# Two cross-attentions on one core: weights and x laid out in long runs, a bias row loaded early, and the last rounds shared out anew

## The chip, the cores and the metric

The kernel runs on one core of a Trainium2 chip. The metric is the device time of one execution in microseconds (us). The median of three runs of the kernel before the change is 1020.93 us (1020.56 to 1021.36).

## The reference

Two attention layers run one after the other, each with its residual and layer norm. There are 2 batches of 2048 tokens with 512 features, and a context of 128 tokens per batch. Both layers have 16 heads; layer 0 has 64 features per head (1024 in all), layer 1 has 32. All is float32.

```python
def layer0(x, ctx, mask):
    q = x @ Wq + bq;  k = ctx @ Wk + bk;  v = ctx @ Wv + bv          # 16 heads of 64
    a = (q . k) * mask
    a = exp(a - max(a over everything)) * mask
    a = a / (sum(a over keys) + 1e-15)
    return layernorm((a . v) @ Wo + bo + x) * gamma + beta

def layer1(y, ctx):
    q = y @ Wq.T;  k = ctx @ Wk.T;  v = ctx @ Wv.T                   # 16 heads of 32
    a = softmax(q . k / sqrt(32) over keys)
    return layernorm((a . v) @ Wo.T + bo + y) * gamma + beta

out = layer1(layer0(x, ctx, mask), ctx)
```

## The kernel before

The 4096 tokens are cut into eight blocks t = 0 to 7 of TB = 512 tokens (four to a batch). NQ = 4 row tiles of 128 tokens make a block, and NG = 4 groups g of four heads make the heads. The order of the work is written out by hand: each engine (PE for matmuls, DVE, ACT, POOL, and SP, which issues nearly all transfers) runs its own queue in the order of the program, so an instruction that waits holds up all behind it on its engine.

**Buffers.** A pool hands out its buffers of one tag in turn; a tile that takes a buffer waits until the last reader of the tile that had it is done. Tags that matter here: "q" (4 buffers of 128x512: queries, later the reciprocal rows r, and before the change the row bo1), "z" (8 buffers: value biases bv0, the sums t1, t2, t4 of tokens, later the residual rows), "mm" and "av" (two PSUM banks each), "sc0" and "sc1" (two double banks of PSUM for scores and maxima).

**The opening (L208 to L254).** The transposed context cT goes out on ACT's queue, the key weights wk0, x and the query weights wq0 on SP's, the masks on POOL's. The weights come from DRAM as 128-row chunks of their rows. Layer 0's weights wk0 and wq0 are fetched in parts, because the first groups are needed first; `load_x(t)` fetches the transposed block t in two halves. `row` (L131) fetches a row and spreads it over 128 partitions.

**Layer 0's steps (L477 to L532).** i = 0 to 15 runs over pairs of blocks p and groups g. Each step makes queries of two blocks for one group, and their scores; the probabilities and values of the step before come in between. `keys0(e)` makes the keys of two heads (e = 0 to 7, two of them per group). At i = 0 the queries are four plain products (`queries0`, L329); from i = 1 on `queries_pair` (L348) makes four query tiles with seven products out of sums of weights and tokens, and DVE adds them up (L360, L362). `scores0` (L396) multiplies with keys and DVE (L408) masks and takes a maximum; each maximum goes to DRAM ("top") and comes back spread over all partitions ("every"). `exponentials0` reduces it on DVE, takes the exponential on ACT (L433), and masks on POOL (L434). `attend0` sums (den, L444) and multiplies with values (psu, L452). At i = 4 the weights of layer 1's keys and values are fetched, and then this:

```python
                bo1s = row(four, bo1, "bo1", "q")
                nc.gpsimd.tensor_tensor(b0s, b0s, bo1s, ALU.add)
```

The bias of layer 1's output is thus folded into the beta of layer 0, which the residual of layer 1 goes through.

**Rounds (L878 to L932).** From then on `steps(t)` lists what round t does, for t = -1 to 7. Letters stand for functions: X `maxima` (L693), M `turn_maxima` (L736), S `scores1` (L766, in the last round also L773), P1 `exponentials1` (L790), V `attend1` (L809), C `divide1` (L820), E `project1` (L831), Y `rest1` (L838, adds the residual), I `moments1`, O `norm1` (ACT L846, POOL L849 and L852), W `store` (L868); T `turn` (L662), Q `queries1` (L680) and Pr `project0` (L629) belong to the next block's layer 0 and queries. In the lists n = t + 1, l = t - 1. `moments1` calls `statistics` (L608): bn on DVE, rstd on POOL (L616), and, if scaled, a shift on POOL (L621). Round 6 makes the queries of block 7, the scores of block 6, and projects rows 0 and 1 of block 5. Round 7 has no next block: it projects rows 2 and 3 of block 5 and all rows of block 6 between the maxima and the scores of block 7.

**The last rows (L949 to L963).** Block 7's four rows are projected, the first half of the groups for all rows first. Row 0 is normed by ACT (`whiten1`) and POOL (`gamma1`, `beta1`), rows 1 to 3 by two DVE operations each (`norm1_vector`, L861 and L864).

Of the kernel before, what the change touches and what calls it, by code (L numbers as in the profile page):

```python
# [9 lines left out]
F32 = mybir.dt.float32  # L10
# [6 lines left out]
P = 128  # L17
# [7 lines left out]
def two_cross_attentions(  # L25
# [29 lines left out]
    K = maskT.shape[1]  # L55
    E = wq0.shape[1]
    H = 16
# [62 lines left out]
    wide = const.tile([P, 2 * ND, TB], F32, tag="wide", name="wq0")  # L120
    wq0s = wide.rearrange("p c m -> p (c m)").rearrange("p (c m) -> p c m", c=ND)

    def chunks(w):
        return w.rearrange("(c p) m -> p c m", p=P)

    def columns(pool, v, name, queue=nc.sync):
        sb = pool.tile(list(v.shape), F32, tag=name, name=name)
        queue.dma_start(sb, v)
        return sb
# [75 lines left out]
    with tc.tile_pool(name="w1", bufs=1) as w1, tc.tile_pool(name="a2", bufs=2) as a2, tc.tile_pool(  # L205
# [3 lines left out]
        first = w1.tile([P, 2 * ND, TB], F32, tag="first", name="wk0")  # L209
        wk0s = first.rearrange("p c m -> p (c m)").rearrange("p (c m) -> p c m", c=ND)  # L210
        W = 2 * P

        for c in (slice(0, 2), slice(2, 4)):
            nc.scalar.dma_start(cTs[:, c, :], chunks(cT)[:, c, :])
            nc.sync.dma_start(wk0s[:, c, :P], chunks(wk0)[:, c, :P])
        nc.sync.dma_start(wk0s[:, :, P : 2 * P], chunks(wk0)[:, :, P : 2 * P])
        nc.sync.dma_start(wk0s[:, :, 2 * P : 4 * P], chunks(wk0)[:, :, 2 * P : 4 * P])
        bk0s = columns(w1, bk0, "bk0", nc.scalar)
        bq0s = columns(w1, bq0, "bq0", nc.scalar)

        def load_x(t):

            b, q0 = where(t)
            pool, tag = (big, "big") if t // 2 % 2 else (xs, "xt")
            tiles = []
            for h in range(2):
                xt = pool.tile([P, 2, TB], F32, tag=tag, name=f"xt_{t}_{h}")
                rows = xT[b, 2 * h * P : 2 * (h + 1) * P, q0 : q0 + TB]
                nc.sync.dma_start(xt, rows.rearrange("(c p) q -> p c q", p=P))
                tiles.append(xt)  # L230
            xts[t] = tiles
# [8 lines left out]
        masks = {0: load_mask(0), 1: load_mask(1)}  # L240
        load_x(0)
        wv0s = []
        for n in range(E // W):
            at = slice(n * W, (n + 1) * W)
            if n == 1:
                load_x(1)
                for c in range(ND):
                    w = big.tile([P, 2, TB], F32, tag="big", name=f"wv0_{c}")
                    wv0s.append(w.rearrange("p n q -> p (n q)"))
                    nc.sync.dma_start(wv0s[c], wv0[c * P : (c + 1) * P, :])  # L250
                bv0s = [row(eight, bv0[:, n * TB : (n + 1) * TB], f"bv0_{n}", "z") for n in range(E // TB)]
            nc.sync.dma_start(wq0s[:, :, at], chunks(wq0)[:, :, at])
            if n > 1:
                nc.sync.dma_start(wk0s[:, :, at], chunks(wk0)[:, :, at])  # L254

# [3 lines left out]
        def keys0(e):  # L259
            ps = mm_tile(f"psk0_{e}")  # L260
            for c in range(ND):
                nc.tensor.matmul(  # L262
                    ps[:, : B * K], wk0s[:, c, e * P : (e + 1) * P], cTs[:, c, :],
                    start=(c == 0), stop=(c == ND - 1),
                )
# [21 lines left out]
        def halves0(g):  # L287
            return [
                [wq0s[:, 2 * k : 2 * k + 2, (2 * g + m) * P : (2 * g + m + 1) * P] for k in range(2)]
                for m in range(2)  # L290
            ]
# [34 lines left out]
        def queries0(t, e):  # L326
            ps = mm_tile(f"psq0_{t}_{e}")
            for c in range(ND):
                nc.tensor.matmul(  # L329
                    ps, wq0s[:, c, e * P : (e + 1) * P], xts[t][c // 2][:, c % 2, :],  # L330
                    start=(c == 0), stop=(c == ND - 1),
                )
# [129 lines left out]
        bo0s, g0s, b0s = row(const, bo0, "bo0"), row(const, g0, "g0"), row(const, b0, "b0")  # L462
        g1s, b1s = row(const, g1, "g1"), row(const, b1, "b1")
        b0cs = columns(const, b0c, "b0c")
        g0cs = columns(const, g0c, "g0c")
# [11 lines left out]
        for i in range(len(order) // 2):  # L477
            p, g = i // NG, i % NG
            steps0 = order[2 * i : 2 * i + 2]
            if g == (2 if p == 0 else 1) and p + 1 < NB // 2:  # L480
                for t in (2 * p + 2, 2 * p + 3):
                    load_x(t)
                    masks[t] = load_mask(t)
            if p == 0 and g != 1:
                for e in range(4) if g == 0 else (2 * g, 2 * g + 1):
                    keys0(e)
# [3 lines left out]
            if i == 4:  # L490
                w = w1.tile([P, 2 * ND, TB], F32, tag="first", name="wkv1")
                wk1s, wv1s = w[:, :ND, :], w[:, ND:, :]
                nc.sync.dma_start(wk1s, chunks(wk1))
                nc.sync.dma_start(wv1s, chunks(wv1))
                bo1s = row(four, bo1, "bo1", "q")
                nc.gpsimd.tensor_tensor(b0s, b0s, bo1s, ALU.add)
            if i == 12:
# [380 lines left out]
    def steps(t):  # L878
        n, f, l = t + 1, t + 2, t - 1
        if n == NB:  # L880
            return [
                (X, t, 0), (V, l, 3), (E, l - 1, 2), (Y, l - 1, 2), (I, l - 1, 2), (X, t, 1), (E, l - 1, 3),
                (Y, l - 1, 3), (I, l - 1, 3), (O, l - 1, 2), (X, t, 2), (E, l, 0), (Y, l, 0), (I, l, 0),
                (O, l - 1, 3), (W, l - 1, 2), (X, t, 3), (E, l, 1), (M, t), (Y, l, 1), (I, l, 1), (O, l, 0),
                (W, l - 1, 3), (E, l, 2), (Y, l, 2), (I, l, 2), (O, l, 1), (W, l, 0), (S, t, 0), (E, l, 3),
                (Y, l, 3), (I, l, 3), (O, l, 2), (W, l, 1), (S, t, 1), (V, t, 0), (C, t, 0), (O, l, 3),
                (W, l, 2), (S, t, 2), (V, t, 1), (C, t, 1), (S, t, 3), (V, t, 2), (C, t, 2), (W, l, 3),
                (V, t, 3), (C, t, 3),
            ]
# [30 lines left out]
        if n == NB - 1:  # L920
            return start + [
                (T, n), (M, t), (O, l, 0), (Q, n, 0), (O, l, 1), (Q, n, 1), (S, t, 0), (P1, t, 0),
                (Q, n, 2), (S, t, 1), (P1, t, 1), (V, t, 0), (W, l, 0), (Q, n, 3), (S, t, 2), (P1, t, 2),
                (V, t, 1), (W, l, 1), (S, t, 3), (P1, t, 3), (V, t, 2),
            ]
# [26 lines left out]
    for i in range(NQ):  # L952
        project1(t, i, 1)
        if i == 1:
            whiten1(t, 0)
            gamma1(t, 0)
        rest1(t, i)
        moments1(t, i, i == 0)
    beta1(t, 0)
    for i in (0, 3, 1, 2):  # L960
        if i:
            norm1_vector(t, i)
        store(t, i)  # L963
# [52 lines left out]
```

## Time and profile before

| | |
|---|---|
| median of three runs | 1020.93 us |
| profiled execution | 1018.7 us, its span 1016.9 us |
| mean granted clock of PE | 0.991 |
| PE busy | 984.1 us, 97% of the span |
| DVE, POOL, ACT busy | 619.3, 471.6, 385.4 us |
| DMA | 127.12 MB, 125 GB/s in the mean |
| chain that ended last | PE 84%, DVE 6%, issue 4%, DMA 3%, ACT 2%, POOL 1% |

All views come from one profiled execution; its times are us from the start of the span. A timeline line reads: start, busy time, engine, line of the kernel, operation, output <- inputs, shapes, count, and in brackets the idle time of that engine just before with what ended it. A line of the waits reads: who waited <- for whom: total us, times, longest us. A line of the window table reads: stretch, its length, the busy time (and count) of PE, of PE's weight loads, of DVE, ACT and POOL, then the clock that PE was granted (1.00 is full), the share of the 16 DMA engines that was busy, and the GB/s moved. PEq, SPq and so on are the queues that issue.

### The profile page before, as it was taken

The page shows a single profiled execution, that of the slowest core. Times are in us where ns is not written, and L with a number is a line of the kernel's source. Part 1 is how long each engine was busy: PE and PEld are TensorE (multiplying, and loading weights), DVE is VectorE, ACT ScalarE, POOL GpSimd, SP SyncE. Part 2 cuts the span into 40 slices and gives each one's busy share as a digit, 9 for nine tenths or more (in the row PEclk, how much of TensorE's full clock was granted, in tenths as well). Part 3 has the DMA queues.
Part 4 walks back from the last instruction along what each step waited for, and adds up shares of the span by engine and source line. Part 5 has one row for each costly group of instructions (what it writes and reads, how often), then busy time and mean ns, then how long its engine had stood idle before and what let it go on. Part 6 is the DMA issues. An engine that isn't in the chain of part 4 may idle for free.

```text
span 1016.9 us, 12273 instructions
## 1 busy us (share of the span) xinstructions
PE 984.1 (97%) x4484; PEld 423.8 (42%) x4484; DVE 619.3 (61%) x965; ACT 385.4 (38%) x622; POOL 471.6 (46%) x392
## 2 busy tenths in 40 slices
PE   8999969999999999999999999999999999999895
PEld 5444323333333334464544444344344344343332
DVE  2544634565564454149569569579488497595767
ACT  1133324333344344134434433434444344344250
POOL 0043244444334445692624925826736547443152
PEclk9999979999999999999999999999999999999998
DMA  9324244214232533642632632713714624204111
GB/s 332 123 53 156 54 140 136 79 53 148 62 79 58 162 120 122 202 134 73 253 121 83 235 99 85 269 64 110 267 64 154 215 85 183 91 1 178 63 53 41
DMA packets 56427, 127.12 MB, mean 125 GB/s; under 512 B 9424, under 2 KB 18384, under 8 KB 52784
## 3 DMA queue, kind: packets, MB, share of 16 engines
q1 hardware_dynamic: 54384, 123.72, 36.3%
q0 software_dynamic: 1152, 2.10, 0.7%
q8 instruction: 35, 0.57, 0.2%
q10 hardware_dynamic: 832, 0.53, 0.2%
q14 instruction: 24, 0.20, 0.1%
HBM read 100.15 MB, written 26.18 MB: 124 GB/s over the span
## 4 chain that ended last, share of the span: by engine, by line
PE 84%; DVE 6%; issue 4%; DMA 3%; ACT 2%; POOL 1%; SPq 0%; POOLq 0%; ACTq 0%; DVEq 0%
PE pso L629 21%; PE ps L348 15%; PE pso L831 10%; PE psq_None L680 8%; PE st L396 6%; PE psu L452 5%; PE mx L693 3%; PE s L766 3%; PE den L444 3%; PE u L809 3%; PE psq L680 2%; PE psq L329 1%; PE psv L274 1%; PE psk L262 1%; DVE p L785 1%
## 5 line engine op out<-in xcount | busy, mean ns | idle before, releaser
L434 POOL TENSOR_TENSOR sm<-sm,mask 128x1024 f32<-128x1024 f32 x64 | 150.1, 2369 | 212.7 <-ACT sm L433 212.7
L629 PE MATMUL pso<-wo,uT 128*128 128x512 f32 x512 | 229.3, 599 | 0.4 <-POOL uT L181 0.4
L616 POOL TENSOR_TENSOR rstd<-rstd,mhalf 128x1 f32<-128x1 f32 x64 | 35.7, 558 | 253.3 <-DVE shift L620 251.9
L629 PEld LDWEIGHTS pso<-wo,uT 128*128 128x128 f32 x512 | 94.3, 190 | 120.7 <-issue 115.3
L831 PE MATMUL pso<-wq,ctx 128*128 128x512 f32 x256 | 114.7, 599 | 0.0
L408 DVE CUSTOM_DVE_ANT_1 sm<-st,mask 128x1024 f32<-128x1024 f32 x64 | 75.9, 1222 | 52.2 <-PE st L396 31.0
L785 DVE TENSOR_TENSOR p<-s,p 128x1024 f32<-128x1024 f32 x56 | 66.0, 1219 | 60.8 <-PE s L766 53.4
L709 ACT ACTIVATE e<-mx,less 128x128 f32<-128x128 f32 x224 | 61.0, 383 | 103.8 <-DVE less L706 103.8
L433 ACT ACTIVATE sm<-sm,ncs 128x1024 f32<-128x1024 f32 x64 | 69.8, 1139 | 72.9 <-DVE ncs L430 72.7
L360 DVE TENSOR_TENSOR q<-ps,q 128x512 f32<-128x512 f32 x75 | 51.5, 689 | 68.8 <-ACT sm L433 31.7
L680 PE MATMUL psq_None<-yT,wq 128*128 128x512 f32 x192 | 88.4, 604 | 1.1 <-ACT yT L669 1.1
L348 PE MATMUL ps<-xt,wq 128*128 128x512 f32 x180 | 83.4, 599 | 0.0
L790 ACT ACTIVATE p<-p 128x2048 f32<-128x2048 f32 x28 | 53.5, 1911 | 73.1 <-DVE p L785 38.7
L181 POOL TENSOR_TENSOR uT<-uT,r 128x1024 f32<-128x1024 f32 x32 | 75.1, 2358 | 6.6 <-DMA r<-r 6.0
L396 PE MATMUL st<-q,k 64*128 64x512 f32 x256 | 65.1, 624 | 8.2 <-DVE q L360 8.0
L831 PEld LDWEIGHTS pso<-wq,ctx 128*128 128x128 f32 x256 | 46.8, 190 | 57.1 <-issue 50.9
L723 DVE TENSOR_REDUCE sums<-e 128x16 f32<-128x2048 f32 x28 | 63.8, 2277 | 1.1 <-ACT e L717 1.1
L452 PE MATMUL psu<-sm,v 128*32 128x512 f32 x512 | 64.1, 607 | 0.0
L699 DVE TENSOR_REDUCE tops<-mx 128x8 f32<-128x1024 f32 x32 | 39.1, 1222 | 29.7 <-PE mx L693 29.7
L348 PE MATMUL ps<-t,s 128*128 128x512 f32 x120 | 56.4, 592 | 0.0
L446 ACT COPY dens<-den 128x512 f32<-128x512 f32 x32 | 18.8, 588 | 98.5 <-PE den L444 98.5
L680 PEld LDWEIGHTS psq_None<-yT,wq 128*128 128x128 f32 x192 | 34.6, 189 | 51.0 <-issue 46.0
(127 smaller groups left out, 1332.2 us busy)
## 6 DMA issues: line engine op xcount, KB each, us to landing
p<-rows SPq DMA_DIRECT2D x28, 1024.0 KB
u<-u SPq DMA_DIRECT2D x32, 512.0 KB
uT<-u SPq DMA_DIRECT2D x32, 512.0 KB
xt<-in_xT_dram SPq DMA_DIRECT2D x16, 512.0 KB
z<-in_x_dram SPq DMA_DIRECT2D x32, 256.0 KB
r<-r SPq DMA_DIRECT2D x32, 256.0 KB
out_dram<-y SPq DMA_DIRECT2D x32, 256.0 KB
r<-rows SPq DMA_DIRECT2D x28, 256.0 KB
```

The costliest lines, as they stand in the source:

```text
L181: nc.gpsimd.tensor_tensor(u, u, r.unsqueeze(1).to_broadcast([P, 2, TB]), ALU.mult)
L348: nc.tensor.matmul(ps, w[:, c, :], x[c] if isinstance(x, tuple) else x[:, c, :], start=(c == 0), stop=(c == 1),)
L396: nc.tensor.matmul(st[n][:, j, :], k0[rows, 2 * g + n, b * K : (b + 1) * K], q[rows, :], start=True, stop=True,)
L408: nc.vector.tensor_tensor_reduce(out=sm, in0=st[n], in1=masks[t].unsqueeze(1).to_broadcast([P, 2, TB]), scale=1.0, scalar=-3.4028234e38, o ...
L433: nc.scalar.activation(s, s, AF.Exp, bias=ncs[:, i + n : i + n + 1])
L434: nc.gpsimd.tensor_tensor(s, s, masks[t].unsqueeze(1).to_broadcast([P, 2, TB]), ALU.mult)
L452: nc.tensor.matmul(ps[32 * j : 32 * (j + 1), :], v0[:, b, d : d + 32], p[j], start=True, stop=True,)
L629: nc.tensor.matmul(ps, uTs[t, n // 2][:, n % 2, i * P : (i + 1) * P], wo0s[n // 2][:, n % 2, :], start=(n == 0), stop=(n == NE - 1),)
L680: nc.tensor.matmul(ps[:, at], wq1s[:, c, g * P : (g + 1) * P], yTs[t][:, c, at], start=(c == 0), stop=(c == ND - 1),)
L723: nc.vector.tensor_reduce(to.rearrange("p r i o -> p r (i o)"), open_x.pop((t, g)), AX.X, ALU.add)
L785: nc.vector.tensor_tensor(p1[:, at], ps[n], p1[:, at], ALU.subtract)
L831: nc.tensor.matmul(ps, ctxs[t][:, g, i * P : (i + 1) * P], wo1s[:, g, :], start=(g == 0), stop=(g == NG - 1),)
```

## The change

1. The host lays out wk0 and wq0 by group of 256 columns, x by block and half, cT by partition, so that one transfer of a partition is one run: 2 KB (wk0 group 0 in halves, cT) or 4 KB (the other weight groups, x) instead of 512 bytes, 1 KB or 2 KB. In SBUF the weights lie group by group.
2. Ahead of the first queries only group 0 of wk0 is fetched and only keys 0 and 1 are made; keys 2 and 3 are made at i = 1.
3. The row bo1 is fetched before x(1), into a "z" buffer, and added before the first step.
4. Rows 2 and 3 of block 5 are projected in round 6; round 6 turns the maxima before it turns the next block; round 7 has two projections fewer.
5. Of block 7, rows 0 and 1 are normed by ACT and POOL, rows 2 and 3 by DVE.

```diff
     wide = const.tile([P, 2 * ND, TB], F32, tag="wide", name="wq0")
-    wq0s = wide.rearrange("p c m -> p (c m)").rearrange("p (c m) -> p c m", c=ND)
+    wq0s = wide.rearrange("p c m -> p (c m)").rearrange("p (n c m) -> p n c m", n=NG, c=ND)
...
-        W = 2 * P
         for c in (slice(0, 2), slice(2, 4)):
-            nc.scalar.dma_start(cTs[:, c, :], chunks(cT)[:, c, :])
-            nc.sync.dma_start(wk0s[:, c, :P], chunks(wk0)[:, c, :P])
-        nc.sync.dma_start(wk0s[:, :, P : 2 * P], chunks(wk0)[:, :, P : 2 * P])
-        nc.sync.dma_start(wk0s[:, :, 2 * P : 4 * P], chunks(wk0)[:, :, 2 * P : 4 * P])
+            nc.scalar.dma_start(cTs[:, c, :], cT[:, c, :])
+            nc.sync.dma_start(wk0s[:, 0, c, :], wk0[:, 0, c, :])
...
-                rows = xT[b, 2 * h * P : 2 * (h + 1) * P, q0 : q0 + TB]
-                nc.sync.dma_start(xt, rows.rearrange("(c p) q -> p c q", p=P))
+                nc.sync.dma_start(xt, xT[b, q0 // TB, h])
...
         load_x(0)
+        nc.sync.dma_start(wq0s[:, 0], wq0[:, 0])
+        bo1s = row(eight, bo1, "bo1", "z")
+        load_x(1)
         wv0s = []
-        for n in range(E // W):
-            at = slice(n * W, (n + 1) * W)
-            if n == 1:
-                load_x(1)
-                for c in range(ND):
-                    w = big.tile([P, 2, TB], F32, tag="big", name=f"wv0_{c}")
-                    wv0s.append(w.rearrange("p n q -> p (n q)"))
-                    nc.sync.dma_start(wv0s[c], wv0[c * P : (c + 1) * P, :])
-                bv0s = [row(eight, bv0[:, n * TB : (n + 1) * TB], f"bv0_{n}", "z") for n in range(E // TB)]
-            nc.sync.dma_start(wq0s[:, :, at], chunks(wq0)[:, :, at])
-            if n > 1:
-                nc.sync.dma_start(wk0s[:, :, at], chunks(wk0)[:, :, at])
+        for c in range(ND):
+            w = big.tile([P, 2, TB], F32, tag="big", name=f"wv0_{c}")
+            wv0s.append(w.rearrange("p n q -> p (n q)"))
+            nc.sync.dma_start(wv0s[c], wv0[c * P : (c + 1) * P, :])
+        bv0s = [row(eight, bv0[:, n * TB : (n + 1) * TB], f"bv0_{n}", "z") for n in range(E // TB)]
+        for n in range(1, NG):
+            nc.sync.dma_start(wk0s[:, n], wk0[:, n])
+            nc.sync.dma_start(wq0s[:, n], wq0[:, n])
...
         g1s, b1s = row(const, g1, "g1"), row(const, b1, "b1")
+        nc.gpsimd.tensor_tensor(b0s, b0s, bo1s, ALU.add)
...
-            if p == 0 and g != 1:
-                for e in range(4) if g == 0 else (2 * g, 2 * g + 1):
+            if p == 0:
+                for e in (2 * g, 2 * g + 1):
                     keys0(e)
...
-                bo1s = row(four, bo1, "bo1", "q")
-                nc.gpsimd.tensor_tensor(b0s, b0s, bo1s, ALU.add)
...
         if n == NB:
             return [
-                (X, t, 0), (V, l, 3), (E, l - 1, 2), (Y, l - 1, 2), (I, l - 1, 2), (X, t, 1), (E, l - 1, 3),
-                (Y, l - 1, 3), (I, l - 1, 3), (O, l - 1, 2), (X, t, 2), (E, l, 0), (Y, l, 0), (I, l, 0),
-                (O, l - 1, 3), (W, l - 1, 2), (X, t, 3), (E, l, 1), (M, t), (Y, l, 1), (I, l, 1), (O, l, 0),
-                (W, l - 1, 3), (E, l, 2), (Y, l, 2), (I, l, 2), (O, l, 1), (W, l, 0), (S, t, 0), (E, l, 3),
-                (Y, l, 3), (I, l, 3), (O, l, 2), (W, l, 1), (S, t, 1), (V, t, 0), (C, t, 0), (O, l, 3),
-                (W, l, 2), (S, t, 2), (V, t, 1), (C, t, 1), (S, t, 3), (V, t, 2), (C, t, 2), (W, l, 3),
-                (V, t, 3), (C, t, 3),
+                (X, t, 0), (V, l, 3), (W, l - 1, 3), (X, t, 1), (E, l, 0), (Y, l, 0), (I, l, 0), (X, t, 2),
+                (E, l, 1), (Y, l, 1), (I, l, 1), (O, l, 0), (X, t, 3), (E, l, 2), (Y, l, 2), (I, l, 2),
+                (O, l, 1), (W, l, 0), (M, t), (E, l, 3), (Y, l, 3), (I, l, 3), (O, l, 2), (W, l, 1),
+                (S, t, 0), (O, l, 3), (W, l, 2), (S, t, 1), (V, t, 0), (C, t, 0), (S, t, 2), (V, t, 1),
+                (C, t, 1), (W, l, 3), (S, t, 3), (V, t, 2), (C, t, 2), (V, t, 3), (C, t, 3),
             ]
...
         if n == NB - 1:
             return start + [
-                (T, n), (M, t), (O, l, 0), (Q, n, 0), (O, l, 1), (Q, n, 1), (S, t, 0), (P1, t, 0),
-                (Q, n, 2), (S, t, 1), (P1, t, 1), (V, t, 0), (W, l, 0), (Q, n, 3), (S, t, 2), (P1, t, 2),
-                (V, t, 1), (W, l, 1), (S, t, 3), (P1, t, 3), (V, t, 2),
+                (E, l, 2), (O, l, 0), (M, t), (Y, l, 2), (I, l, 2), (T, n), (O, l, 1), (Q, n, 0), (O, l, 2),
+                (Q, n, 1), (S, t, 0), (P1, t, 0), (W, l, 0), (Q, n, 2), (S, t, 1), (P1, t, 1), (V, t, 0),
+                (W, l, 1), (Q, n, 3), (S, t, 2), (P1, t, 2), (V, t, 1), (W, l, 2), (E, l, 3), (Y, l, 3),
+                (I, l, 3), (S, t, 3), (P1, t, 3), (V, t, 2), (O, l, 3),
             ]
...
     for i in range(NQ):
         project1(t, i, 1)
+        rest1(t, i)
+        moments1(t, i, i < 2)
+        if i < 2:
+            whiten1(t, i)
         if i == 1:
-            whiten1(t, 0)
             gamma1(t, 0)
-        rest1(t, i)
-        moments1(t, i, i == 0)
-    beta1(t, 0)
-    for i in (0, 3, 1, 2):
-        if i:
+        if i == 2:
+            beta1(t, 0)
+    gamma1(t, 1)
+    beta1(t, 1)
+    for i in (0, 2, 3, 1):
+        if i > 1:
             norm1_vector(t, i)
         store(t, i)
...
+    def fours(w):
+        return w.reshape(w.shape[0] // P, P, -1, 2 * P).transpose(1, 2, 0, 3)
...
-        "xT": x.transpose(0, 2, 1),
-        "cT": cx.reshape(-1, cx.shape[-1]).T,
+        "xT": x.reshape(x.shape[0], -1, TB, 2, 2, P).transpose(0, 1, 3, 5, 4, 2),
+        "cT": cx.reshape(-1, cx.shape[-1] // P, P).transpose(2, 1, 0),
...
-        "wq0": a["L0_xattn_Wq"],
+        "wq0": fours(a["L0_xattn_Wq"]),
...
-        "wk0": a["L0_xattn_Wk"],
+        "wk0": fours(a["L0_xattn_Wk"]),
```

More of the change, by code (lines that the diff above doesn't have):

```diff
@@ L55, in two_cross_attentions @@
     K = maskT.shape[1]
-    E = wq0.shape[1]
+    E = wv0.shape[1]
     H = 16
@@ L209, in two_cross_attentions @@
         first = w1.tile([P, 2 * ND, TB], F32, tag="first", name="wk0")
-        wk0s = first.rearrange("p c m -> p (c m)").rearrange("p (c m) -> p c m", c=ND)
-        W = 2 * P
+        wk0s = first.rearrange("p c m -> p (c m)").rearrange("p (n c m) -> p n c m", n=NG, c=ND)
         for c in (slice(0, 2), slice(2, 4)):
-            nc.scalar.dma_start(cTs[:, c, :], chunks(cT)[:, c, :])
-            nc.sync.dma_start(wk0s[:, c, :P], chunks(wk0)[:, c, :P])
-        nc.sync.dma_start(wk0s[:, :, P : 2 * P], chunks(wk0)[:, :, P : 2 * P])
-        nc.sync.dma_start(wk0s[:, :, 2 * P : 4 * P], chunks(wk0)[:, :, 2 * P : 4 * P])
+            nc.scalar.dma_start(cTs[:, c, :], cT[:, c, :])
+            nc.sync.dma_start(wk0s[:, 0, c, :], wk0[:, 0, c, :])
         bk0s = columns(w1, bk0, "bk0", nc.scalar)
@@ L262, in keys0 @@
                 nc.tensor.matmul(
-                    ps[:, : B * K], wk0s[:, c, e * P : (e + 1) * P], cTs[:, c, :],
+                    ps[:, : B * K], wk0s[:, e // 2, c, (e % 2) * P : (e % 2 + 1) * P], cTs[:, c, :],
                     start=(c == 0), stop=(c == ND - 1),
@@ L288, in halves0 @@
             return [
-                [wq0s[:, 2 * k : 2 * k + 2, (2 * g + m) * P : (2 * g + m + 1) * P] for k in range(2)]
+                [wq0s[:, g, 2 * k : 2 * k + 2, m * P : (m + 1) * P] for k in range(2)]
                 for m in range(2)
@@ L329, in queries0 @@
                 nc.tensor.matmul(
-                    ps, wq0s[:, c, e * P : (e + 1) * P], xts[t][c // 2][:, c % 2, :],
+                    ps, wq0s[:, e // 2, c, (e % 2) * P : (e % 2 + 1) * P], xts[t][c // 2][:, c % 2, :],
                     start=(c == 0), stop=(c == ND - 1),
```

## The prediction

> **What bounds the kernel now.** I read the page first (busy shares and slices), then the waits of TensorE (PE), the chain that ended last in order of time, timelines of the stretches where PE is not full, and the window table for clock and DMA.
>
> ```profile
> PE   8999969999999999999999999999999999999895
> PEclk9999979999999999999999999999999999999998
> ```
>
> Each digit is a slice of 25.4 us. PE is full but in the first, the sixth (127 to 152), the third from the end and the last. PE's work is the same before and after, so only these places can give time. The sixth slice also has a low clock. The waits (total us, times, longest) name its cause:
>
> ```profile
> PE st L396 <- DVE q L360: 8.0, 1, 8.0
> POOL b L496 <- DMA bo<-in_bo_dram: 25.1, 1, 25.1
> DVE q L360 <- POOL b L496: 9.9, 1, 9.9
> ```
>
> Read upward: at i = 4 GpSimd (POOL) waits for the row bo1, VectorE (DVE) for POOL, PE for DVE. The row sits in a "q" buffer, so the fourth query tile of i = 4 can't be written until POOL has added it. The chain in order of time (start us, us, what) shows the price:
>
> ```profile
> 135.66 1.27 POOL b L496
> 138.96 2.08 PE st L396 x4
> 141.04 2.48 PE den L444 x8
> 143.52 2.59 PE psu L452 x16
> ...
> 150.80 12.21 PE ps L348 x28
> ...
> 163.01 1.92 PE st L396 x8
> 165.93 1.77 PE psu L452 x16
> ...
> 172.39 12.21 PE ps L348 x28
> ```
>
> A plain step lasts 172.39 - 150.80 = 21.59 us. Step i = 4 runs from its first query product at 117.58 (timeline) to 150.73: 33.15 us, 11.56 too long. Of this 8.04 is the wait (130.92 to 138.96); 3.4 is the slow clock behind it: half the scores, sums and values take 7.15 us (138.96 to 146.11) where 0.96 + 1.00 + 1.77 = 3.73 is usual.
>
> **The early row: -11.56.** It goes into a "z" buffer before the first step. Its DMA (0.64 us of SP time at 126.39) leaves step 4's queue, its addition (1.27 us on POOL) goes to about 30 us, where POOL is idle until 49.80. "q" then rotates as in every other step. New wait: the ninth "z" tile (the last t4 of token_sums_2, on DVE at 41.76) takes bo1's buffer and so needs the addition, and that the row b0, issued at 25.46. Behind it on DVE stand weight sums and the additions that empty the values' PSUM, and PE needs both. Some ten us of slack: I cost it at nothing; without them a later b0 costs one for one. What is late next in step 4? The two 1 MB loads wk1 and wv1 stay (124.88, 125.35) and drain by some 134.5. The first top of step 4 now leaves near 133.4 and must come back from DRAM ("every") for step 5, which starts at 117.58 + 21.59 = 139.2. Its sum matmuls, 14.1 later, need a reduction (0.6), an exponential (1.1) and two POOL products (4.7) behind it, so it may land until 146. Write (111.88 to 115.00 in step 3) and read, about 3 each, end at 139.5. It fits.
>
> **The opening: +1.4.** SP waits for an earlier DMA before each new issue, which dates the landings:
>
> ```profile
> 12.62 1.83 SPq L133 DMA_DIRECT2D bv<-in_bv_dram  x2
> 14.12 0.33 SPq L133 DMA_DIRECT2D bv<-in_bv_dram  x1
> 15.47 0.38 SPq L252 DMA_DIRECT2D wq<-in_wq_dram  x1
> ```
>
> Its waits name xt, wq, xt: the second half of x(0) landed at 12.62, group 0 of wq0 at 14.12, half of x(1) at 15.47. The first query matmul starts at 14.24. (The page names ACT's fourth key, ended at 14.20, but its PSUM tile is not the one needed; in later steps no such wait appears.) So the first query waits for the queue, 3.67 MB: cT 0.52, wk0 1.05, masks 0.52, x(0) 1.05, wq0 0.52. From 14.24 to 117.6 PE has no idle time, so everything is worth what it shifts this start.
>
> Group 1 of wk0, 0.52 MB, leaves the front: 1.4 us (12.62 to 14.12 to 15.47). Long runs: DMA moved
>
> ```profile
> 5.00:8.00 3.00, 1.86 (x8) 1.12 (x6) 0.11 (x1) 0.35 (x1) 0.00 (x0) 1.00 1.13 293
> 9.00:14.00 5.00, 4.69 (x22) 3.69 (x20) 0.17 (x1) 1.64 (x4) 0.00 (x0) 1.00 1.06 382
> 16.00:20.00 4.00, 4.00 (x11) 1.81 (x10) 0.00 (x0) 0.69 (x1) 0.00 (x0) 1.00 1.03 410
> ```
>
> (from the window table; last column GB/s) 293 while 512-byte runs of wk0 were under way, 382 with x in 2 KB runs, 410 with wv0 in 4 KB runs. After, 3.15 MB stand ahead. By the table in steps of 1 us 0.48 MB had moved at 4 us; the other 2.67 MB at 395 (between the last two rows) take 6.8 us, and the landing lags the bytes by 1.0 (3.67 MB had moved at 13.1). wq0 then lands at 11.8 to 12, the first query starts at 12.0: -2.2. But keys 2 and 3 now come behind it, on a PE with no gap: one pair costs 3.65 (chain, "67.57 3.65 PE psk L262 x16"). Net +1.4; bounds +0.5 (410 GB/s, no lag beyond 0.3) and +2.1 (no gain by runs, landing at 12.7).
>
> The Trainium skill, "DMA: Bandwidth & Descriptors", Specifications, sets line rate from 512 bytes a run; by it longer runs bring nothing, the opening costs +2.1 and the whole sum is 0.7 higher. The row at 293 speaks against it here, though masks and broadcasts mix in.
>
> Other moved loads (bo1 before x(1); wk0 before wq0 in each group) have cover: x(1) lands near 16 and is needed near 21, group 1 of wq0 near 24 for DVE's sums at 22 to 24, where DVE has 2 to 3 us before its scores at 29. Chunk order in SBUF changes no instruction count.
>
> **Rounds 6 and 7: 0.** Two projections (3.63 us each) with additions, moments, norms and stores move from round 7 to 6. SP holds only stores there behind the last r load, so they block no load. Before, PE idles from 917 to 950.4:
>
> ```profile
> 918.23 1.20 PE L662 MATMUL tr_None<-ident,z 128*128 128x128 f32 x9 [0.65 <-ACT z L644]
> 920.10 0.66 PE L662 MATMUL tr_None<-ident,z 128*128 128x128 f32 x4 [0.67 <-ACT yT L669]
> 935.72 1.06 PE L809 MATMUL u<-p,v 128*32 128x512 f32 x8 [0.86 <-ACT p L790]
> 943.46 2.26 PE L766 MATMUL s<-q,k 32*128 32x512 f32 x8 [0.98 <-DVE p L785]
> 946.58 1.06 PE L809 MATMUL u<-p,v 128*32 128x512 f32 x8 [0.86 <-ACT p L790]
> 949.45 1.06 PE L809 MATMUL u<-p,v 128*32 128x512 f32 x8 [0.69 <-ACT p L790]
> ```
>
> 4.7 in brackets, and about 1 more inside each of the two score groups of 2.2 (1.14 otherwise): 6.8. After: project(5,2) at 917.1, maxima turned at 921, tT copied on DVE by 923.1; the third transpose waits for that "av" tile, the fourth for project(5,2)'s addition, ACT whitens (5,0) before it empties the first transpose (923.2): queries start at 924.7, about as late as 921.0 + 3.6. Then nothing stalls up to V2 (950.1); but the addition and moments of project(5,3) (1.75 us) now stand before the last p (2.36) on DVE, so maxima wait until 952.3, values g = 3 for the exponentials until 954.3, the second maxima for DVE until 956. By then PE has won 2.4. Round 7 has lost two fillers: the second scores follow the first directly and wait for ACT's two exponentials (1.94): they end at 979.65, against 977.71 + 1.93. Net 0. Bounds: -2.8 (the waits of round 7 don't form), +1.2 (0.65 and 0.67 come back doubled).
>
> **The last rows: -0.1.** Now rows 1, 2, 3 end on DVE (six operations of 0.75) and row 0 on ACT and POOL; after, rows 0 and 1 take ACT and POOL, DVE keeps four.
>
> ```profile
> 1008.15 0.74 DVE L861 SCALAR_TENSOR_TENSOR y<-y,mv,g 128x512 f32<-128x512 f32 x1
> 1008.32 0.99 POOL L616 TENSOR_TENSOR rstd<-rstd,mhalf 128x1 f32<-128x1 f32 x1 [1.25 <-DVE rstd L615]
> 1009.27 1.26 POOL L852 TENSOR_TENSOR y<-y,b 128x512 f32<-128x512 f32 x1
> 1009.34 1.74 DVE L864 SCALAR_TENSOR_TENSOR y<-y,rstd,b 128x512 f32<-128x512 f32 x1 [0.44 <-POOL rstd L616]
> ```
>
> Side by side, the DVE operation took 1.74 for 0.75 and POOL's rstd 0.99 for 0.55: the second of each pair ended 0.55 and 0.42 after the first. If they take turns from 1008.67 (end of POOL's beta for row 0): DVE 0.6, rstd 0.4, DVE 0.6, gamma 1.2, DVE 0.6, beta 1.2, DVE 0.6 = 5.2, end 1013.9, against 1013.98. Without the turns DVE would end by 1011.4 and POOL by 1011.9, -2.1. I take -0.1, the row's own case; bounds -2.1 and +0.5.
>
> The Trainium skill, "SBUF — State Buffer", Who interferes with whom, says that DVE with two SBUF inputs and GpSimd reading SBUF hold one port pair exclusively, a whole instruction at a time; it speaks against this part, and the 1.74 agrees. By a rule of free overlap the sum would be 2.0 lower.
>
> **Sum.** -11.56 + 1.4 + 0 - 0.1 = -10.3. The profiled execution took 1018.7 (span 1016.9) and would take 1008.4; the median, 1020.93, is 2.2 above it, so 1010.6.
>
> **Rivals.**
> - The end overlaps better (rounds -2.8, last rows -2.1, or both): 1010.6 less 2.1 to 4.9, 1005.7 to 1008.5. For it: 6.8 us of idle PE to win. Against: DVE's order and the 1.74. Chance 0.2.
> - The clock falls in the opening: PE's two keys end near 9.2 (the second halves of cT and wk0 land near 6.5, an estimate from SP's issue at 6.04; 0.9 and 1.8 follow), the first query is at 12.0, 2.8 us idle. In step 4 the clock (0.50 from 136 to 144) fell 4 us after PE stopped, at the end 2.6 us after; a fall here costs up to the 3.4 of step 4: 1012.5 to 1014. Chance 0.13.
> - Slower: the 2 MB of wk1 and wv1 take the row's place. DVE's reduction over "every" stands in front of the query additions; if "every" of step 4 lands after 146, each us later is one lost, and beyond 146 + 10.3 = 156.3 the kernel is slower; at 159, as long after the burst as the row held POOL (25), by 2.7: 1023.6. Against: DMA is empty by 136 in the trace. Chance 0.02.
> - The wait isn't removed (a "q" buffer held by something else): 1020.93 + 1.3, 1022.2. The diff leaves no other "q" tile among the queries: 0.02.
>
> Forecast 0.63. The range takes in the first two rivals for the most part: 1006.5 to 1013.4. A measurement here tells 0.2%, 2.0 us. Faster by more: 0.96; within: 0.02; slower: 0.02.
>
> **What would show it.** Right: no POOL wait for bo near 110 to 136, clock 1.00 in slice 6, step 4 at 21.6; first query near 12, keys of 3.65 in step 1; PE idle moved to maxima of round 7; DVE and POOL alternating at the end. Wrong: first query before 10.4 (the opening gains), step 4 over 23, DVE's last operations at 0.75 beside POOL, or PE at half clock near 12.

## The result and the profile after

The changed kernel took 1010.45 us in the median (1009.07 to 1011.88, four runs), the kernel before 1020.74 us (1019.21 to 1021.36, four runs): a ratio of 0.9902 [0.9884, 0.9919]. The forecast was 1010.6 us.

The profiled execution took 1010.61 us, its span is 1008.8 us. Against the profiled execution of before that is 8.1 us less, not 10.3. Profiles of single executions of this kernel differ by a few us, and the sections below say why; so both differences are kept in view.

The page's rows for PE and for its clock:

```profile
PE   9999999999999999999999999999999999999995
PEclk9999999999999999999999999999999999999898
```

The hole in the sixth slice is gone, in PE and in the clock. PE is full from the first slice on. New is a dip of the clock in the third slice from the end (slice 38). The waits of PE were headed by 8.0 us for the query tile. They are now headed by 2.1 us of values u (L803) for ACT, and then this:

```profile
PE mx L687 <- DVE p L779: 1.7, 2, 1.0
```

The second lies wholly in round 7; of the first only 0.49 us does. The wait of POOL for the row bo1 (25.1 us at step 4) is no more; POOL's one long wait in the opening is for the row b0 (31.4 us, the addition at 34.12), with nothing behind it on POOL until 50.90.

The chain of waits in order of time (start, us, what), cut to the stations that matter:

```profile
11.90 7.11 PE psq L324 x16
...
36.97 3.45 PE psk L257 x16
47.29 12.02 PE ps L343 x28
...
118.77 12.21 PE ps L343 x28
...
141.00 5.30 DMA top<-top
146.32 5.23 DMA every<-top
...
162.68 12.21 PE ps L343 x28
```

Line by line: the first query starts at 11.90 (before 14.24). One pair of keys, 3.45 us, now stands at the start of step 1, and step 1's first pair product starts at 47.29 (before 46.18). Steps 4 and 5 together last 162.68 - 118.77 = 43.91 us, two plain steps 43.18 (21.59 each): 0.73 us came back, and the chain names the second maximum's way to DRAM and back. From 162.68 on nothing stands between the steps.

So the pair of profiles adds up as follows, by the starts that the timeline gives (it has step 4 of the change at 118.70 and step 6 at 162.61, 0.07 ahead of the chain). Start of step 4: 117.58 to 118.70, +1.12. Steps 4 and 5: 54.74 to 43.91, -10.83. From step 6 to the first projection of block 5 (910.12 and 900.25): -0.16. From there to the last block's projections (991.98 and 983.92): 81.86 to 83.67, +1.81. From there to the end of the span: 24.92 to 24.88, -0.04. Sum -8.1. The 2.2 us between this and the medians lie nearly all in the execution of before that was profiled: 1018.7 us, where its four runs beside the change took 1019.21 to 1021.36.

Round 7 in the timeline of PE, and four us of it in the window table (stretch, length, busy time and count of PE, PE's weight loads, DVE, ACT, POOL, granted clock, DMA share, GB/s):

```profile
941.01 0.49 PE L687 MATMUL mx<-k,q 32*128 32x128 f32 x4 [1.04 <-DVE p L779]
942.14 1.50 PE L687 MATMUL mx<-k,q 32*128 32x128 f32 x28 [0.64 <-DVE p L779]
944.13 1.93 PE L803 MATMUL u<-p,v 128*32 128x512 f32 x8 [0.49 <-ACT p L784]
...
948.20 4.40 PE L825 MATMUL pso<-wq,ctx 128*128 128x512 f32 x8
```

```profile
942.00:946.00 4.00, 3.37 (x36) 1.41 (x36) 3.01 (x4) 2.61 (x2) 1.14 (x1) 0.60 0.00 0
```

The maxima wait for DVE's last p and the values for ACT, as the prediction had it. But 2.17 us of waits between 939.97 and 944.13 were followed by a slower clock (0.60 in the row, 0.55 from 946 to 950): values of 1.93 instead of 1.06, a projection of 4.40 instead of 3.70, and between them maxima of 2.09 instead of 1.17. These three take 2.49 us more; the other waits of the stretch are shorter than in before, and +1.81 is left.

The last rows (timeline of DVE and POOL, in order of time):

```profile
1001.74 1.75 DVE L855 SCALAR_TENSOR_TENSOR y<-y,mv,g 128x512 f32<-128x512 f32 x1
1003.02 1.59 POOL L846 TENSOR_TENSOR y<-y,b 128x512 f32<-128x512 f32 x1
1003.59 1.57 DVE L858 SCALAR_TENSOR_TENSOR y<-y,rstd,b 128x512 f32<-128x512 f32 x1
```

DVE and POOL take turns: DVE's operations take 1.75 and 1.57 us where one alone takes 0.75, and the last one ends 0.55 after POOL's.

### The profile page after: what moved, and what is told of

The parts are those of the page before. It is cut to its first block, busy times and chain, and to the rows that moved or that the text cites. A ratio compares the mean times of both kernels' runs of the same rounds, so it can differ in the third digit from the quotient of the medians.

```text
span 1008.8 us, 12279 instructions
## 1 busy us (share of the span) xinstructions
PE 985.0 (98%) x4484; PEld 426.3 (42%) x4484; DVE 619.2 (61%) x964; ACT 386.4 (38%) x623; POOL 474.8 (47%) x395
## 4 chain that ended last, share of the span: by engine, by line
PE 88%; DVE 5%; DMA 3%; ACT 2%; issue 1%; POOL 0%; SPq 0%; DVEq 0%; ACTq 0%; POOLq 0%
PE pso L623 21%; PE ps L343 17%; PE pso L825 10%; PE psq_None L674 8%; PE st L391 6%; PE psu L447 5%; PE mx L687 3%; PE s L760 3%; PE den L439 3%; PE u L803 3%; PE psq L674 2%; PE psk L257 2%; PE psq L324 1%; PE psv L269 1%; ACT yT L663 1%
## 5 line engine op out<-in xcount | busy, mean ns | idle before, releaser
L343 PEld LDWEIGHTS ps<-xt,wq 128*128 128x128 f32 x180 | 33.2, 190 | 46.5 <-issue 44.0
```

Source lines behind the costliest of these rows:

```text
L343: nc.tensor.matmul(ps, w[:, c, :], x[c] if isinstance(x, tuple) else x[:, c, :], start=(c == 0), stop=(c == 1),)
```

## The experiments

Theory: the early row is the whole gain; the opening gives a part of it back, because the keys that left the front stand in a step where PE has no gap; the other two parts are nought, and what they seem to cost is the clock. Rival: the parts add up otherwise (the lists of rounds 6 and 7 cost by their order, the long runs or the last rows gain). Kernels that are compared with the same time of before ran on the same chip.

### Each part alone, put into the kernel before

**row_only**: the row goes into a "z" buffer early; nothing else.

```diff
             if n == 1:
+                bo1s = row(eight, bo1, "bo1", "z")
                 load_x(1)
...
+        nc.gpsimd.tensor_tensor(b0s, b0s, bo1s, ALU.add)
...
-                bo1s = row(four, bo1, "bo1", "q")
-                nc.gpsimd.tensor_tensor(b0s, b0s, bo1s, ALU.add)
```

> Only the early bias row, all else as before. Theory (the wait for the row is the whole gain): steps 4 and 5 together fall from 33.15 + 21.59 us to 43.2 plus some 0.7 that comes back because the second maximum of step 4 is late, so the kernel is 10.5 to 11.6 us faster than before, more than the whole change. Rival (the loads of wk1 and wv1 hold step 4 as well): step 4 stays above 25 us and the gain is below 8.

Measured 1007.68 us against 1019.8, ratio 0.9873 [0.9856, 0.9890]: 12.1 us, more than the whole change (between the two profiled spans, 1016.9 and 1006.0, it is 10.9). The stretch that held the hole, in the window table of this kernel:

```profile
127.00:152.00 25.00, 25.00 (x101) 9.09 (x99) 11.90 (x23) 9.14 (x12) 10.43 (x6) 1.00 0.53 172
```

In before PE was busy for 16.96 of these 25 us at a mean clock of 0.80; here it is full at 1.00. The addition on POOL runs at 35.46, before t4 needs its buffer.

**opening_only**: weights, x and cT in long runs, the new order of loads, keys 2 and 3 at i = 1; the row stays late.

> Only the new layouts, the new order of the first loads and keys 2 and 3 at step 1; the bias row stays late. Theory: first query near 11.9 instead of 14.24, step 1's first pair product near 47.3 instead of 46.18, so 1.1 us slower. Rival (long runs and the earlier query pay): equal or faster by up to 1.

Measured 1021.44 against 1019.8, ratio 1.0008 [0.9996, 1.0021]. The interval does not exclude nought, but the trace shows a loss: the first pair product of step 1 starts at 49.50 (before 46.18). The first query in the timeline of PE, and the clock while it runs, in the window table:

```profile
12.41 8.80 PE L323 MATMUL psq<-xt,wq 128*128 128x512 f32 x16 [3.37 <-issue]
```

```profile
14.00:16.00 2.00, 2.00 (x4) 0.86 (x3) 0.00 (x0) 0.00 (x0) 0.00 (x0) 0.50 1.02 418
```

This is the rival that the prediction gave 0.13: the two keys end at 9.05, PE is idle for 3.37 us, the clock falls (0.71 from 12 to 14, then 0.50), and the queries take 8.80 instead of 7.11. The profiled execution of the full change does not show it. There the two keys ran slowly and ended only at 11.67:

```profile
5.04 6.63 PE L257 MATMUL psk<-cT,wk 128*128 128x256 f32 x16 [0.74 <-DMA cT<-in_cT_dram]
```

The slow keys cost nothing there, since wq0 landed at 11.83, and they left PE no long idle stretch.

**rounds_only**: the new lists of rounds 6 and 7.

> Only the new lists of rounds 6 and 7. Theory (the clock falls in round 7's waits whenever they form): the last block's projections start 1.8 us later relative to round 6's first projection than before (81.9 us apart before, 83.7 with the whole change), and the kernel is 1 to 2 us slower. Rival (the fall of the clock was chance in the one profile): no fall, apart by 81.5 to 82, no difference in time.

Measured 1020.85 against 1019.8, ratio 1.0004 [0.9993, 1.0015]: no difference that can be told. In its profile the distance from block 5's first projection to the last block's projections is 84.02, with a fall of the clock in the waits of round 7 as in the full change.

**tail_only**: the new last rows.

> Only the new sharing of the last four rows. Theory (DVE and POOL take turns on operands in SBUF): from the end of PE to the end of DVE 7.2 us instead of 8.0, so 0.3 to 0.8 us faster. Rival (they overlap): 2 us faster.

Measured 1019.53 against 1019.8, ratio 0.9990 [0.9979, 1.0000]. From the last block's projections to DVE's last end the new order saves 0.76 us (7.24 instead of 8.00 after PE's end), but the span ends as late: 10.87 after PE's end against 10.92. The waits of the store queue say where the 0.7 went:

```profile
SPq L868 <- DVE y L864: 3.9, 2, 2.9
```

The stores go out in the order of rows 0, 2, 3, 1. Row 1, done on POOL ahead of DVE's last operation, stands behind row 3, whose store waits 2.9 us for DVE (the longest such wait in before was 1.0); so two rows are left to go out at the end, where it was one. The traffic after DVE's last operation agrees: 0.52 MB from 1014.8 to 1016.2, in before one store from 1014.8 to 1015.5.

### One part taken back, in the changed kernel

**old_rounds**: the lists of rounds 6 and 7 as before.

> The changed kernel with the old lists of rounds 6 and 7. Theory (the new lists lose in round 7, by waits and a fall of the clock): the last block's projections begin 81.9 us after round 6's first projection as before, not 83.7, and the kernel gains 1 to 2 us over the changed one, near 0.9885 of before. Rival (the new lists cost nothing, the one profile was unlucky): same as the changed kernel, 0.990.

Measured 1010.16 against 1020.39, ratio 0.9901 [0.9883, 0.9920]; the changed kernel 0.9902. The distance is 83.12, with the clock down in round 6 this time. So a fall is not the new lists' own.

**keys_in_front**: wk0's group 1 ahead of x(0), keys 2 and 3 ahead of the first queries, as before the change; long runs kept.

```diff
             nc.sync.dma_start(wk0s[:, 0, c, :], wk0[:, 0, c, :])
+        nc.sync.dma_start(wk0s[:, 1], wk0[:, 1])
...
-            if p == 0:
-                for e in (2 * g, 2 * g + 1):
+            if p == 0 and g != 1:
+                for e in range(4) if g == 0 else (2 * g, 2 * g + 1):
```

> The changed kernel, but group 1 of wk0 is fetched before x(0) again and keys 2 and 3 come before the first queries, still in long runs. Theory (what costs is the pair of keys behind the first query, what gains are the long runs): wq0 lands 1.3 us later than in the changed kernel, the four keys fill the wait, first query near 13.3, step 1's first pair product near 45.3 instead of 47.3; about 1 to 2 us faster than the changed kernel. Rival (the keys can't start earlier than DMA lets them, and at half clock they end later than wq0): first query at 14.3 or later, no gain over 1 us.

Measured 1008.58, ratio 0.9887 [0.9867, 0.9906]; with the keys at step 1, old_rounds took 1010.16 and warm_round7 (below) 1010.44 on the same chip. The intervals of the three ratios overlap, so the trace has to carry the reading. PE in the opening:

```profile
10.55 3.72 PE L259 MATMUL psk<-cT,wk 128*128 128x256 f32 x16 [1.56 <-ACT k L263]
14.11 7.03 PE L326 MATMUL psq<-xt,wq 128*128 128x512 f32 x16
```

The four keys fill the time until wq0 lands; the query starts 2.2 us later than in the change, but no key stands in step 1, and its first pair product starts at 45.97 instead of 47.29.

**short_runs**: the old layouts in DRAM, the new order of loads kept.

> The changed kernel with x, cT, wk0 and wq0 laid out in DRAM as before (runs of 1 and 2 KB), the new order kept. Theory (the fewer bytes ahead and the longer runs both count): first query at 12.6 to 12.9 instead of 11.9, the kernel 0.5 to 1 us slower than the changed one. Rival (from 512 bytes a run the length makes no difference): 11.9 again and no difference.

Measured 1012.06, ratio 0.9917 [0.9896, 0.9937]; on the same chip the same order with long runs took 1010.16 (old_rounds, with the old lists). The profiled execution was the slowest of its six (1014.43). Three us of the opening in the window table:

```profile
5.00:8.00 3.00, 2.79 (x13) 2.13 (x13) 0.10 (x1) 0.00 (x0) 0.00 (x0) 1.00 1.05 263
```

The DMA engines moved 263 GB/s at a busy share of 1.05; in the change, in the same window, 380 at 1.09. The first query starts at 13.21 instead of 11.90, 1.3 later, so the theory's direction came true. But the 1 KB runs are not where the time goes. The slow part is 6 to 8 us (235 and 178 GB/s); the keys ran from 6.11 without another wait, so cT and wk0 had landed, and all packets of these two us are either shorter than 512 bytes or at least 2 KB long. From 9 to 13 us, while wq0 came in 1 KB runs (512 packets of 512 to 2047 bytes), it was 385 GB/s. The old layouts as a whole go with the later query; which of their transfers is slow, and why, is open. PE had been idle for 4.24 us, and the clock fell here as in opening_only (queries 9.79 instead of 7.11): the pair product at 51.28.

**warm_round7**: three matmuls whose result nobody reads, in round 7's waits.

```diff
-                (X, t, 0), (V, l, 3), (W, l - 1, 3), (X, t, 1), (E, l, 0),
+                (warm, t, 2), (X, t, 0), (V, l, 3), (W, l - 1, 3), (warm, t, 1), (X, t, 1), (E, l, 0),
```

> The changed kernel with three matmuls whose results nobody reads put into round 7's waits, two before the first maxima and one after the values of g = 3 (0.86 us each). Theory (half of the loss there is the clock): the granted clock stays at 1.00 between 942 and 950, values and second maxima take 1.1 and 1.2 us instead of 1.9 and 2.1, and the last block's projections begin 81.6 to 82.4 us after round 6's first projection instead of 83.7; 1 to 2 us faster. Rival (the waits alone cost): 83.7 or more, slower by the part of the 2.6 us of matmuls that no wait covers.

Measured 1010.44, ratio 0.9906 [0.9889, 0.9923]. The profile shows what was meant: clock 1.00 in round 7, values of 1.06, maxima of 1.17, distance 82.05 instead of 83.67. The time did not move: the profiled execution had steps 4 and 5 at 44.11, and by the ratios (0.9906 and 0.9902, each good to some 1.8 us) the timed executions of the change do not seem all to have paid the 1.6 us of its profile.

### What is left, and a better mix

**best_mix**: keys_in_front with the old lists. What stays of the change is the early row, the long runs and the new last rows.

> The changed kernel with the lists of rounds 6 and 7 as before, wk0's group 1 loaded ahead of x(0) and keys 2 and 3 in front of the first queries: the early row, the long runs and the new last rows are what is left of the change. If the parts add up: row -12.1 (measured alone), long runs about -1 (first pair product of step 1 at 46.0 where the early row alone had 46.96), last rows -0.1 to -1, lists 0: about 1006.5 to 1007.5, that is 3 us below the changed kernel and below the early row alone. Rival, that the long runs give nothing once the keys are in front (queue time only moved): first pair product at 47.0 and 1007.7. Rival, that the new lists did gain and only the clock hid it: 1009 or more.

Measured 1007.39 (1006.52 to 1008.82) against 1020.38, ratio 0.9872 [0.9851, 0.9893]. First pair product at 45.85, as the sum of the parts had it. It beats both kernels: 13.0 us below before, and its slowest run lies below the fastest of the change, though on another chip. Below the early row alone it is not: row_only had 0.9873 (on another chip), row_tail (below) 1.1 us more on this one, and the intervals overlap. That the long runs give something shows in the traces alone: with four keys in front the first pair product starts at 45.85 to 46.16 with them (three kernels) and at 46.18 to 47.45 without (five). Its lists are the old ones, and the clock fell in its round 6 (0.61 from 932 to 936, 0.54 from 936 to 940, distance 83.29), so even this execution had some 1.4 us left.

**best_warm**: the new lists and the three unread matmuls on top of keys_in_front.

> As best_mix, but with the new lists of rounds 6 and 7 and three matmuls that nobody reads in round 7's waits, so that the clock does not fall there. If the fall of the clock in those waits is what the new lists pay for and timed runs pay it too: distance from round 5's first projection to the last block's projections near 82.0, and the time equals best_mix within 0.5 us, some 1.5 us below the kernel with the keys in front and the new lists (1008.6 at its ratio). If the timed runs mostly do not pay it: equal to that kernel, 1008.5, and the lists cost 0.2 to 0.4 by themselves.

Measured 1007.52, ratio 0.9874 [0.9853, 0.9895]: equal to best_mix within 0.2. Clock 0.997, distance 82.08. New lists with the clock held and old lists come out the same.

**row_tail**: row_only with the new last rows.

> The kernel before with the early row and the new last rows alone; opening and lists as before. If the last rows are worth nothing or 0.1, as predicted: the time of the early row alone, ratio 0.987. If they give 0.8 (TensorE's last matmul to VectorE's last operation 7.2 instead of 8.0) less what the order of the stores takes back: ratio 0.9865. If the gain of 1.3 us of the last rows alone was noise: no difference, distance of the last matmul to the end of the span 10.9 in both.

Measured 1008.52, ratio 0.9881 [0.9861, 0.9901]; row_only 0.9873. From PE's end to the end of the span 10.84 here and 10.96 there: the last rows give 0.1. The medians cannot tell so little.

**wkv_later**: the loads of wk1 and wv1 at step 6 instead of step 4, in the changed kernel.

> The changed kernel with the loads of wk1 and wv1 (2 MB) issued at step 6 instead of step 4; nothing else. If the 0.7 us that came back in steps 4 and 5 are those loads in front of the second top of step 4: that top comes back from DRAM some 5 us earlier, VectorE's reduction of it no longer waits, steps 4 and 5 take 43.2 together, and the time falls by 0.5 to 0.7 below the changed kernel. The loads then lie beside steps 6 and 7, whose tops they could delay in the same way: steps 6 and 7 at 43.9 and no gain. Rival, the return is something else than the loads: 43.9 stays in steps 4 and 5.

Measured 1011.35 (1007.82 to 1013.58), ratio 0.9913 [0.9893, 0.9933]: no gain. The profiled execution was the fastest of the six (1007.82) and shows two things. First, DVE's reduction of the second maximum of step 4 (timeline of DVE; the change, then wkv_later):

```profile
151.57 0.42 DVE L424 TENSOR_REDUCE whole<-every 128x2 f32<-128x256 f32 x1 [3.37 <-DMA every<-top]
150.78 0.42 DVE L424 TENSOR_REDUCE whole<-every 128x2 f32<-128x256 f32 x1 [2.57 <-DMA every<-top]
```

Step 4 starts at 118.77 in both, and steps 4 and 5 last 43.91 us in the change and 43.18 here. Over the ten profiles with an early row, the start of this reduction, counted from step 4's first pair product, gives the delay. From 30.89 to 32.08 us (six kernels) nothing is lost; at 32.24, 32.28, 32.80 and 33.00 the two steps take 0.17, 0.22, 0.73 and 0.93 more. So there is a deadline at 32.07, and beyond it each us counts one for one. But the loads are not shown to be the cause. From the issue of the maximum's way to DRAM to the reduction it takes 9.2 to 11.0 us in these profiles, 10.6 in the change and 10.5 with the loads out of the way. So 0.74 of the 0.79 us between the change and wkv_later lie ahead of that. DVE has the second maximum at 139.24 in both, but SP can't send it yet: its queue waits until the first maximum is written, and only then issues that one's way back and, 1.5 us later, the second's way out. The first write took 4.95 us in the change (134.58 to 139.53) and 4.23 in wkv_later; over the ten profiles it takes 3.72 to 5.73, the lowest value with the loads in place (row_tail). Added to the second maximum's trip it puts the ten in the order of the delay. What sets the lengths of the two trips is open.

Second, round 7 here has the change's own list, longer waits, and no fall of the clock:

```profile
940.14 0.49 PE L687 MATMUL mx<-k,q 32*128 32x128 f32 x4 [1.04 <-DVE p L779]
941.27 1.16 PE L687 MATMUL mx<-k,q 32*128 32x128 f32 x28 [0.64 <-DVE p L779]
943.26 1.06 PE L803 MATMUL u<-p,v 128*32 128x512 f32 x8 [0.83 <-ACT p L784]
```

With 0.65 us ahead of the next maxima these are 3.16 us of waits. Values, maxima and the projection behind them run at full speed (1.06, 1.17, 3.70); distance 81.75. The change had 2.17 us of waits in the same place and lost 1.8 us to the clock. Over all profiles the distance is 81.6 to 82.0 with the old lists and 81.75 to 82.1 with the new ones where the clock holds, and 82.6 to 84.0 with either where it falls. It falls in three of the seven profiles with the old lists and in four of the five with the new ones and no added matmuls: too few to say whether the new lists make it likelier.

## Why the prediction was right, by its own steps

That the two medians are 10.3 us apart, as forecast, is partly luck. Their ratio is good to some 1.8 us; the two profiles are 8.1 us apart; and the four parts, each alone against before, add up to -12.1 + 1.6 + 1.1 - 0.3 = -9.7. What the experiments bear out is where the time lies.

**The early row (-11.56): right.** Cause, place and size are shown: alone it gives 12.1 us, and steps 4 and 5 of the full change are 10.83 shorter. The missing 0.7 lie in a step of the argument that went only half its length. The prediction asked what is late next, and dated step 4's first maximum (landed by 139.5, needed by 146). Here a term was too small, without effect: write and read, "about 3 each", took 4.95 and 3.57 us, and the maximum was reduced at 143.10. The second one of the same step was not dated. It stands right behind, on the same queue, and it is the one that comes too late, by 0 to 0.93 us from one execution to the next.

**Cover of the addition: right, the slack smaller.** The addition ran at 34.12, not about 30, and t4 needed the buffer at 39.42. That leaves 4 us, not some ten.

**The opening (+1.4): right in sum and in its parts, the reason for the faster loads not shown.** First query at 11.90 (12.0 was said), one pair of keys 3.45 (3.65), first pair product +1.11. (The lower bound's own figures, 410 GB/s and a lag of 0.3, give about +0.3 and not +0.5; nothing rests on it.) One step was wrong without effect: the keys were to end near 9.2 and ended at 11.67, because they ran at about half their later pace (the last section says why that is put down to the clock). The rival built on the idle time after them happened in opening_only and short_runs, and cost 1.7 and 2.7 us there. As for the rule that the prediction weighed (the Trainium skill, "DMA: Bandwidth & Descriptors", Specifications: line rate from 512 bytes a run): short_runs moved 263 GB/s where long runs moved 380, and its first query came 1.3 later, but its slow us held no 1 KB runs, and where they did run it moved 385. So the runs do not decide on the rule. The time that the prediction put on longer runs came out about right (-2.34 at the first query, where -2.2 was said); that the run length is the reason is not shown.

**Rounds 6 and 7 (0): right in the times, outside its bound in the profile.** The waits went where the prediction put them: maxima for DVE's last p (1.04 and 0.64), values for ACT, and the second scores for ACT's exponentials (1.17, where 1.94 was said). Where the clock holds, the distance is 81.75 to 82.08 with the new lists, against 81.86 in before: -0.1 to +0.2, though two of these three profiles carry the added matmuls. The term that was left out is the clock: some 0.7 to 2.1 us in an execution where it falls, +1.81 in the profile of the change against a bound of +1.2. It falls with the old lists too (opening_only, old_rounds, best_mix), which may be why it does not show in the medians: rounds_only 1.0004.

**The last rows (-0.1): right in the number, partly by luck.** -0.04 in the pair of profiles, -0.1 between row_tail and row_only. The turns of DVE and POOL are there, as the prediction took them from one pair of lines. But they were costed too high: from the end of POOL's beta for row 0 to DVE's end it put 5.2 us and the change took 4.74 (1000.42 to 1005.16), with that beta done 0.2 earlier after PE's end than estimated; so DVE ends 0.76 earlier than before and not 0.1. The stores were not in the sum at all, and their order gives the 0.7 back. Two errors cancel.

**The other rivals.** That the end overlaps better is refuted (the last rows by the turns, the rounds by old_rounds and best_mix). That the 2 MB hold up step 4's first maximum beyond 146 is refuted: it was reduced at 143.10. That the wait isn't removed is refuted by the waits.

**What stays open.** Twenty timed executions of five kernels with four keys in front took 1008.0 us in the mean, twenty of four kernels with long runs and keys at step 1 took 1010.6. The profiles explain 1.3 of the 2.6 for the kernels with long runs, and nothing for row_only and row_tail, whose first pair products (46.96 and 47.45) are hardly earlier than the change's. Their mean clocks were 0.9954 and 0.9943, so part of it is falls of the clock in executions that have no trace; 0.001 of mean clock went with about 0.5 us among the second twenty. That the pause between the keys and the queries is where these falls happen fits opening_only and short_runs, but was not shown for the change itself. Nor is it the chips alone: the two groups differ the same way on each of two chips (1008.58 against 1010.16 and 1010.44; 1007.39, 1007.52 and 1008.52 against 1011.35).

## What to carry to other kernels

When a long wait is removed, date every transfer of the step behind it, not only the first: the next bound was the second of two round trips, sent only once the first was written, with a deadline that ten profiles agree on within 0.1 us. Work moved from a stretch where an engine waits anyway into a stretch where it is full costs its whole length, however much earlier the first piece starts: the keys were free in front of the queries and cost 3.5 us in step 1. An engine that ends earlier gains nothing until the queue behind it, here the stores, lets the span end earlier too.

## What the runs showed of the hardware that was not expected

The clock of PE falls without a long idle stretch. In the change PE was busy 0.00, 0.49, 0.86 and 0.64 of the four us from 940 to 944, and the clock was 0.50 from 943 to 949; in wkv_later waits in the same places and in one more, 0.99 us longer in all, left it at 1.00. In best_mix the clock fell at about 932.9; the last wait that had ended by then was 0.74 us long (to 930.58), and the next, of 0.87, had just begun. The Trainium skill, "TensorE: Matmul & The Clock Gate", Part 1, describes a window of about 3.4 us that runs freely and throttles after an idle one. That it runs freely would fit falls that come and go at the same place of the program; that a whole window must be idle does not agree with these rows, which are nearer to the second case of the same part, short idles between groups of matmuls.

At the start the profile's clock row may not show the pace. From 5 to 8 us it stood at 1.00 both in the change, where PE got through 7 key matmuls, and in keys_in_front, where it got through 13; in the change 16 of them took 6.63 us, and the next 16, at the start of step 1, 3.45. That this is the clock, which starts up late, is inferred.
